# More portions of an edge-count matrix begun in the look-up turns of a graph-network kernel

## The chip, the cores and the metric

The kernel runs on one core of a Trainium2 chip. The metric is device time in microseconds (us) of one execution; the number given for a kernel is the median of several runs. The engines are named as in the profile: PE (TensorE, matrix multiplications; PEld is its weight load), DVE (VectorE), ACT (ScalarE), POOL (GpSimd) and SP (SyncE, which here only issues transfers). Each engine works through its own list of instructions in order and waits at an instruction until what it needs is there.

## What is computed

Four graph layers in a row over 6250 nodes with 64 features and 206,250 edges, each layer fed by a layer norm and a ReLU and added to its input. The edges come sorted by their destination.

```python
h = jnp.maximum(_layernorm(x, axis=-1), 0.0)
x = x + _L0_gnn_ref(h, edge_index, W3, b3, W4, b4)   # two normalized sums over neighbours, 64 -> 128 -> 64
h = jnp.maximum(_layernorm(x, axis=-1), 0.0)
x = x + _L1_gnn_ref(h, edge_index)                   # a normalized sum over neighbours
h = jnp.maximum(_layernorm(x, axis=-1), 0.0)
x = x + _L2_gnn_ref(h, edge_attr_64, src, dst, ...)  # messages per edge, gated by edge features
h = jnp.maximum(_layernorm(x, axis=-1), 0.0)
x = x + _L3_gnn_ref(edge_index, h)                   # three more normalized sums
```

The sum over neighbours, which most layers share, is

```python
deg = jax.ops.segment_sum(w, d, num_segments=n)
dinv = jnp.where(deg > 0, jax.lax.rsqrt(deg), 0.0)
msgs = (dinv[s] * dinv[d])[:, None] * x[s]
agg = jax.ops.segment_sum(msgs, d, num_segments=n)
```

## The kernel before

Nodes are padded to 6272, 49 blocks of 128. The kernel does not gather edge by edge: it builds once the dense matrix of edge counts, source by destination, in 8 bits, and every sum over neighbours is then a matrix product with it. The matrix is built in strips of destinations: 14 strips, alternately 512 and 384 destinations wide (`OF_CHUNK`). A strip stays in on-chip memory (pool `spool`, three buffers) until the first convolution has used it, and is written to main memory (`A`) for the later layers.

A strip is made of **portions** of 32 destinations: 16 portions in a wide strip, 12 in a narrow one, 196 in all. A portion takes two steps:

- `one_hots(s, q, n)` (L882, DVE): two comparisons (both L889), `hd` for the high part of the source and `lo` for its low part, against the keys of the edges that end in these destinations. `n` is 1 for a single portion or 2 for a pair made by one pair of instructions. The results lie in pool `opool`, two buffers.
- `placed(...)` (L896): for each portion sixteen matmuls on PE (L904) count the edges into `p_a` (two buffers of PSUM), and two copies on ACT (L908) put the counts into the strip. After a strip's last portion SP issues the write to `A` (L915).

`whole(s, q)` makes the one-hots of a single portion and puts it on the list `waiting`; `place()` takes all that wait through `placed`.

Everything happens in `first_stage`, where the order of the instructions on PE, DVE, ACT and POOL is the order of the code. It has these parts:

1. **Set-up.** Edge ends are read, packed into pairs (key, low part of the source) and written to main memory.
2. **The prelude**, a loop of 32 turns (L945), `GC` = 25 groups of 128 pairs of destinations running through it as in a pipeline. In turn i POOL issues the look-up `near` of group i (L948); DVE reads the look-up of group i-2 (L954) and finds the exact begin of its runs (L957); POOL issues the look-up `run` of group i-3 (L961); ACT copies the keys of group i-6 (L966) and turns group i-5 into digits (L973, L975), which PE transposes (L978); `place()` (L979) places what was made a turn earlier; after every ninth group and the last, DVE compares the keys (`less`, L987), PE counts them (L991) and DVE copies the counts (`below`, L994). At the end of a turn DVE fills in other work by a **credit** (L997 to L1002): so much credit is added per turn, and items are taken from the list `fill` and charged their cost until it is used up. The list holds the scans that find where each group begins (`scanned`, L866, with `begun_at`, L871) and the parts of the first layer norm (`centred`, `deviation`, `scaled`, L848 to L862). When it is empty, an item is one single portion of the first strip, at a cost of 2.0.
3. **The degrees.** After the loop DVE takes differences of `below` (L1007), PE spreads them (L1010), and from them comes the norm (L1018, L684 to L686). The portions not yet made become the list `jobs`; if their number is odd, one more single portion is made there.
4. **The scaled features**, in three 16-bit parts (`U3`, L1117 to L1124), while PE runs the first unit of the first convolution (L1129).
5. **The main loop** (L1150) over the pairs of portions in `jobs`: DVE makes the one-hots of the next pair while PE and ACT place the present one. After each portion `sums` hands out steps of the convolution (L1044) to PE. A step is one matmul of a block of a strip; there are 2401 steps in units of 98 or 49, and a unit may begin only when its destinations are built. How many steps follow a portion is what is left of them, divided by the portions left plus five. DVE reduces each finished unit (`added`, L1057), and the small operations of the hidden layer (`hidden`, L1078 to L1110) are spread between.

After the first stage come the gathers of the later layers (first matmuls at L1194), which read `A` back piece by piece, the edge stage, and the last layers.

The prelude's credit at L997 and its fallback at L999 read:

```python
credit += 1.4
while credit > 0:
    cost, f, *args = fill.pop(0) if fill else (2.0, whole, 0, singles)
    singles += f is whole
```

Of the kernel before, what the change touches and what calls it, by code (L numbers as in the profile page):

```python
# [593 lines left out]
CS = NP // CW  # L594
# [23 lines left out]
def fast(ctx, tc, bad, x, src, dst, edge_attr, W3, b3, W4, b4, w1, b1, w2, b2, Bw, Bb, Cw, Cb,  # L618
# [140 lines left out]
    def first_stage(ph):  # L759
# [115 lines left out]
        def portions(s):  # L875

            lo, hi = OF_CHUNK[s % 2]
            return (hi - lo) * P // 2 // (2 * SG)
# [43 lines left out]
        def place():  # L922
            while waiting:
                for _ in placed(*waiting.pop(0)):
                    pass
# [4 lines left out]
        fill = [(0.4, scanned, c) for c in range(3, 10)] + [(0.3, begun_at, 3, 10)]  # L930
# [11 lines left out]
        begun_at(0, 3)  # L942

        near_of, run_of, digits_of, credit, singles = {}, {}, {}, 0.0, 0
        for i in range(GC + 7):  # L945
            if i < GC:
                near_of[i] = rpool.tile([P, LOOK, 2], F32, name="near2")
                nc.gpsimd.indirect_dma_start(  # L948
                    out=near_of[i].rearrange("p e t -> p (e t)"), out_offset=None, in_=pairs[:, :],
                    in_offset=bass.IndirectOffsetOnAxis(ap=begin_i[:, i:i + 1], axis=0))  # L950
            if 0 <= i - 2 < GC:
                c = i - 2
                n = rpool.tile([P, 1], F32, name="n")
                nc.vector.tensor_scalar(junk[:, :LOOK], near_of.pop(c)[:, :, 0],  # L954
                                        start_of[:, c:c + 1], 0.0,
                                        op0=OP.is_lt, op1=OP.add, accum_out=n)
                nc.vector.tensor_add(exact_i[:, c:c + 1], begin[:, c:c + 1], n)  # L957
            if 0 <= i - 3 < GC:
                c = i - 3
                run_of[c] = rpool.tile([P, P, 2], F32, name="run")  # L960
                nc.gpsimd.indirect_dma_start(  # L961
                    out=run_of[c].rearrange("p e t -> p (e t)"), out_offset=None, in_=pairs[:, :],
                    in_offset=bass.IndirectOffsetOnAxis(ap=exact_i[:, c:c + 1], axis=0))
            if 0 <= i - 6 < GC:
                c = i - 6
                nc.scalar.activation(key[:, :, c * P:(c + 1) * P],  # L966
                                     digits_of.pop(c)[:, :2 * P].rearrange("p (k s) -> p k s", k=2),
                                     AF.Copy)
            if 0 <= i - 5 < GC:
                c = i - 5  # L970
                run = run_of.pop(c)
                digits = rpool.tile([P, 2, P], BF16, name="digits")
                nc.scalar.activation(digits[:, 0, :], run[:, :, 0], AF.Identity,  # L973
                                     bias=minus[:, c:c + 1])
                nc.scalar.activation(digits[:, 1, :], run[:, :, 1], AF.Copy)  # L975
                p = digits_of[c] = psum.tile([P, 1024], BF16, name="p_dig")
                for k in range(2):
                    nc.tensor.transpose(p[:, k * P:(k + 1) * P], digits[:, k, :], ident_b)  # L978
            place()  # L979
            if 0 <= i - 6 < GC:  # L980
                c = i - 6
                if c % 9 == 8 or c == GC - 1:
                    c0 = c // 9 * 9
                    p = psum.tile([P, 512], F32, name="p_node")
                    for k in range(3):
                        less = rpool.tile([P, 9 * P], BF16, name="less", bufs=2)
                        nc.vector.tensor_scalar(  # L987
                            less[:, :(c + 1 - c0) * P], key[:, 0, c0 * P:(c + 1) * P],
                            float(k * NB), None, op0=OP.is_lt)
                        for i_ in range(c0, c + 1):  # L990
                            nc.tensor.matmul(p[:, k * 9 + i_ - c0:k * 9 + i_ - c0 + 1],  # L991
                                             less[:, (i_ - c0) * P:(i_ - c0 + 1) * P],
                                             count[:, 1, 0:1], start=True, stop=True)
                    nc.vector.tensor_copy(  # L994
                        below[:, :, c0:c + 1],
                        p[:, :27].rearrange("p (k i) -> p k i", k=3)[:, :, :c + 1 - c0])
            credit += 1.4  # L997
            while credit > 0:
                cost, f, *args = fill.pop(0) if fill else (2.0, whole, 0, singles)  # L999
                singles += f is whole  # L1000
                f(*args)
                credit -= cost  # L1002
        assert singles <= portions(0) and not fill

        for h in range(2):
            at = slice(h * D, (h + 1) * D)
# [2 lines left out]
        for k in range(2):  # L1009
            nc.tensor.matmul(p[:, :2 * GC], spread_2[:, k, :],  # L1010
                             deg[:, k].rearrange("p h c -> p (h c)"), start=(k == 0), stop=(k == 1))
        jobs = [(s, q) for s in range(CS) for q in range(portions(s))][singles:]
        place()
        if len(jobs) % 2:
            whole(*jobs.pop(0))
# [156 lines left out]
    with ExitStack() as ph, tc.manual_schedule(  # L1172
            engines={ET.PE, ET.DVE, ET.Activation, ET.Pool}):
        norm0, norm3, V3, b4_r, hidden = first_stage(ph)
# [613 lines left out]
```

## Time and profile before

| | us |
|---|---|
| median of 3 runs | 3474.78 (3472.68 to 3476.98) |
| the profiled execution | 3475.05 |
| its span, first to last instruction | 3473.3 |
| DVE busy in the span | 2451.6 (71%) |
| PE busy in the span | 2702.6 (78%) |
| ACT / POOL busy in the span | 1228.0 / 1602.0 |

| place in the profiled execution | us from the span's start |
|---|---|
| first turn of the prelude on DVE | 23.98 |
| first single portion (L889) | 66.1 |
| degrees (L1007) | 104.93 |
| first pair's one-hots | 121.41 |
| DVE's last pair ends | 516.8 |
| first matmul of the gathers (L1194) | 527.46 |

The first stage takes some 527 of the 3473 us; what follows does not depend on the change but starts when the first stage lets it. Times on the timeline are microseconds from the start of the span; a bracket at the end of a line gives the idle time of that engine before the instruction and what ended it. An instruction's start may lie before the end of its forerunner on the same engine, as they are pipelined: the distance from start to start is what one costs.

### The profile page before, as it was taken

What the parts mean: (1) busy time and instruction counts of PE and PEld (TensorE: products, weight loads), DVE (VectorE), ACT (ScalarE), POOL (GpSimd) and SP (SyncE); (2) the same over time, 40 slices, a digit from 0 to 9 for tenths busy, and PEclk for the clock granted to TensorE, in tenths of its full rate; (3) what the DMA queues carried; (4) which work ended last, traced back from release to release, by engine and by line L of the source; (5) the groups of instructions that cost most, each with busy time, mean ns of one, the idle gap of its engine ahead of it and who ended that gap; (6) DMA issues with size and microseconds to landing.
All of it is one profiled execution on the core that took longest, in us unless ns stands there. A gap on an engine that the chain in (4) does not pass through costs nothing. (4 is left out here: it accounts for less than half of the span.)

```text
span 3473.3 us, 58582 instructions
## 1 busy us (share of the span) xinstructions
PE 2702.6 (78%) x23087; PEld 2113.6 (61%) x23087; DVE 2451.6 (71%) x4776; ACT 1228.0 (35%) x2071; POOL 1602.0 (46%) x1885
## 2 busy tenths in 40 slices
PE   1799999999966666776776777677677677699999
PEld 1688888999944444443443444444344344399999
DVE  6899993532268868978986997997898697641111
ACT  3677770000024433443444344444434344210000
POOL 6000001000047777777777777777777777500000
PEclk9999999999988888898888898899889989899999
DMA  4234347565443322332332333233233322346664
GB/s 134 64 80 109 83 105 254 188 212 178 147 130 91 87 55 69 91 82 70 97 86 79 88 94 82 76 94 82 67 96 90 79 70 79 85 161 200 204 207 146
DMA packets 255434, 389.54 MB, mean 112 GB/s; under 512 B 96409, under 2 KB 169289, under 8 KB 254894
## 3 DMA queue, kind: packets, MB, share of 16 engines
q1 hardware_dynamic: 190542, 320.69, 30.3%
q0 software_dynamic: 54816, 60.71, 8.4%
q10 hardware_dynamic: 9792, 4.31, 0.6%
q8 instruction: 184, 3.01, 0.3%
q14 instruction: 100, 0.82, 0.1%
HBM read 341.34 MB, written 44.21 MB: 111 GB/s over the span
## 5 line engine op out<-in xcount | busy, mean ns | idle before, releaser
L1527 POOL DMA_INDIRECT v<-Vp_dram,src_g x1616 | 1534.6, 950 | 885.0 <-issue 393.8
L1554 PE MATMUL p_bc<-BC,h 128*128 128x256 f32 x1616 | 512.5, 473 | 399.7 <-DVE m L1572 399.6
L1194 PE MATMUL p_acc<-U,piece 128*128 128x192 bf16 x9604 | 802.2, 247 | 2.5 <-DVE zg L1205 2.5
L1194 PEld LDWEIGHTS <-piece 128*128 128x128 fp8e4 x9604 | 796.3, 98 | 8.3 <-issue 7.7
L1554 PEld LDWEIGHTS p_bc<-BC,h 128*128 128x128 f32 x1616 | 363.8, 235 | 612.4 <-issue 511.6
L1205 DVE TENSOR_REDUCE zg<-p_acc 128x128 f32<-128x384 f32 x112 | 56.3, 507 | 494.8 <-PE p_acc L1194 494.3
L1438 DVE SCALAR_TENSOR_TENSOR junk<-p_sum,there 128x2048 bf16<-128x2048 fp8e4 (+1 forms) x112 | 361.9, 3232 | 8.8 <-PE p_sum L1433 8.6
L1580 ACT ACTIVATE m<-m 128x512 bf16<-128x512 f32 x202 | 127.2, 630 | 649.4 <-DVE m L1573 637.5
L908 ACT ACTIVATE strip<-p_a 128x784 fp8e4<-128x784 f32 x392 | 301.0, 821 | 95.5 <-PE p_a L904 87.6
L1571 DVE TENSOR_TENSOR m<-p_bc,v 128x512 f32<-128x512 f32 x202 | 139.4, 690 | 254.1 <-issue 103.2
L1586 DVE TENSOR_SCALAR to<-count,lane 128x128 bf16<-128x128 bf16 x1616 | 290.7, 276 | 0.0
L1594 PE MATMUL p_s<-m,to 128*128 128x192 bf16 x1616 | 195.0, 272 | 95.9 <-DVE H L1608 71.5
L1544 PE MATMUL p<-h,w_d 128*128 128x512 f32 x404 | 221.6, 631 | 60.5 <-ACT h L1548 60.5
L1548 ACT ACTIVATE h<-p,b_c 128x512 f32<-128x512 f32 x404 | 257.3, 695 | 3.8 <-PE p L1544 3.6
L1594 PEld LDWEIGHTS <-to 128*128 128x128 bf16 x1616 | 150.5, 109 | 168.8 <-DVE H L1608 106.5
L751 PE MATMUL p_sum<-piece,U 128*64 128x448 fp8e4 x2016 | 227.5, 366 | 31.6 <-DVE m L1656 25.7
L1561 DVE TENSOR_TENSOR p_bc<-p_bc,bias 128x1024 f32<-128x1024 f32 x202 | 247.5, 1225 | 2.3 <-PE p_bc L1554 1.8
L1566 ACT ACTIVATE p_bc<-p_bc 128x512 f32<-128x512 f32 x202 | 117.6, 582 | 342.6 <-DVE p_bc L1561 336.6
L1044 PE MATMUL p_sum<-U,strip 128*128 128x192 bf16 x2401 | 229.7, 247 | 0.0
L889 DVE TENSOR_TENSOR lo<-count,key 128x4096 bf16<-128x4096 bf16 (+1 forms) x103 | 224.4, 2179 | 0.0
L751 PEld LDWEIGHTS <-U 128*64 128x64 bf16 x2016 | 116.2, 113 | 167.2 <-issue 72.2
L1544 PE MATMUL p<-eT,w_d 128*128 128x512 f32 x404 | 214.7, 614 | 0.0
(206 smaller groups left out, 3081.0 us busy)
## 6 DMA issues: line engine op xcount, KB each, us to landing
piece<-A SPq DMA_DIRECT2D x243, 784.0 KB
e<-in_edge_attr SPq DMA_DIRECT2D x202, 256.0 KB
v<-Vp_dram,src_g POOLq DMA_INDIRECT x1616
A<-strip SPq DMA_DIRECT2D x7, 3136.0 KB
there<-A SPq DMA_DIRECT2D x196, 112.0 KB
A<-strip SPq DMA_DIRECT2D x6, 2352.0 KB
piece<-A SPq DMA_DIRECT2D x7, 448.0 KB
A<-strip ACTq DMA_DIRECT2D x1, 2352.0 KB
```

Of the source, the lines that this page charges most:

```text
L751: nc.tensor.matmul(p[half * D:(half + 1) * D, :w], U3[:, b, k, :], at_block, start=(i < 2), stop=(i >= 3 * n - 2))
L908: nc.scalar.activation(strips[s][:, :, col:col + 2 * SG].rearrange("p b (j l) -> p b j l", l=2), p[:, :, :2 * NB].rearrange("p j (b l) -> ...
L1044: nc.tensor.matmul(p[:, d * 3 * D:(d + 1) * 3 * D], strips[s][:, b, (d0 - lo + d) * P:(d0 - lo + d + 1) * P], U3[:, b, :, :].rearrange("p ...
L1194: nc.tensor.matmul(p[d // 2][:, d % 2 * 3 * D:(d % 2 + 1) * 3 * D], t[:, b, d * P:(d + 1) * P], U3[:, k * CB + b, :, :].rearrange("p t f - ...
L1438: nc.vector.scalar_tensor_tensor(junk[:m, :a1 - a0], p[:m, :a1 - a0, :].bitcast(COUNT).rearrange("p a (r j) -> p a r j", j=4), 15.5, of_th ...
L1527: ask = nc.gpsimd.indirect_dma_start(out=v[:, j, :], out_offset=None, in_=Vp_dram[:, :], in_offset=bass.IndirectOffsetOnAxis(ap=src_g[:, g ...
L1544: nc.tensor.matmul(of[g][p], w, of[g].pop(x), start=True, stop=True)
L1548: nc.scalar.activation(of[g][t], of[g].pop(p), **how)
L1554: last_of = nc.tensor.matmul(p_bc[:, 2 * q:2 * q + 2].rearrange("p j o f -> p (j o f)"), h2[:, q * P:(q + 1) * P], BC, start=True, stop=True)
L1561: nc.vector.tensor_tensor(p_bc, p_bc, bias.unsqueeze(1).to_broadcast([P, J, 2, D]), op=OP.add)
L1586: nc.vector.tensor_scalar(to[:, j, :], count, lane[:, g, j:j + 1], None, op0=OP.is_equal)
L1594: nc.tensor.matmul(p, to[:, j, :], m3[:, j].rearrange("p t f -> p (t f)"), start=(j == 0), stop=(j == J - 1))
```

## The change

The credit of a prelude turn goes from 1.4 to 2.0. The list of all portions, `jobs`, is made before the loop instead of after it, and the fallback item takes the next portion of this list, whichever strip it belongs to, where before it was always one of strip 0. After the loop the portions made are cut off the list as before. The bound in the assertion is widened to the first two strips.

```diff
         near_of, run_of, digits_of, credit, singles = {}, {}, {}, 0.0, 0
+        jobs = [(s, q) for s in range(CS) for q in range(portions(s))]
         for i in range(GC + 7):
...
-            credit += 1.4
+            credit += 2.0
             while credit > 0:
-                cost, f, *args = fill.pop(0) if fill else (2.0, whole, 0, singles)
+                cost, f, *args = fill.pop(0) if fill else (2.0, whole, *jobs[singles])
                 singles += f is whole
                 f(*args)
                 credit -= cost
-        assert singles <= portions(0) and not fill
+        assert singles <= portions(0) + portions(1) and not fill
...
-        jobs = [(s, q) for s in range(CS) for q in range(portions(s))][singles:]
+        jobs = jobs[singles:]
         place()
         if len(jobs) % 2:
             whole(*jobs.pop(0))
```

## The prediction

> **What bounds the kernel now.** I began with the busy table of the whole span, but its shares average stages with different limits, so the next view was the busy time by stretch, cut at the borders of the first stage. (Columns: the stretch, its length, then busy us and instruction counts of PE, PEld, DVE, ACT and POOL, the granted clock, the DMA share and GB/s.)
>
> ```profile
> core 0: us, PE busy (x) PEld busy (x) DVE busy (x) ACT busy (x) POOL busy (x), PEclk, DMA share, GB/s
> 24.00:66.00 42.00, 7.25 (x53) 3.58 (x53) 32.60 (x138) 15.97 (x51) 31.83 (x32) 1.00 0.30 87
> 66.00:105.00 39.00, 19.81 (x216) 15.76 (x216) 26.85 (x54) 23.69 (x54) 18.03 (x18) 1.00 0.20 59
> 105.00:121.40 16.40, 10.64 (x99) 9.97 (x100) 13.42 (x30) 9.49 (x17) 0.00 (x0) 1.00 0.00 1
> 121.40:516.90 395.50, 367.22 (x5322) 340.84 (x5320) 390.11 (x245) 298.01 (x399) 1.14 (x2) 0.98 0.38 95
> ```
>
> The main loop over pairs of portions (121.4 to 516.9) is DVE's: 390.1 of 395.5 us busy. In the prelude's turns with one-hots (66 to 105) no engine is full; DVE idles 12.2 of 39 us. So the change moves work from a place where DVE is the limit to one where something else is. What that is, the timeline of one turn shows (start, length, engine, line).
>
> ```profile
> 72.76 0.39 ACT L966 ACTIVATE key<-p_dig 128x256 bf16<-128x256 bf16 x1
> 73.02 0.42 ACT L973 ACTIVATE digits<-run,minus 128x128 bf16<-128x128 f32 x1
> ...
> 73.32 0.32 ACT L975 ACTIVATE digits<-run 128x128 bf16<-128x128 f32 x1
> ...
> 73.50 0.49 PE L978 MATMUL p_dig<-ident_b,digits 128*128 128x128 bf16 x2 [1.54 <-ACT digits L973]
> ...
> 73.78 1.51 PE L904 MATMUL p_a<-hd,lo 128*128 128x98 bf16 x16
> ...
> 74.67 1.54 ACT L908 ACTIVATE strip<-p_a 128x784 fp8e4<-128x784 f32 x2 [1.03 <-PE p_a L904]
> ...
> 76.10 0.39 ACT L966 ACTIVATE key<-p_dig 128x256 bf16<-128x256 bf16 x1
> ```
>
> The reader is to see a ring between ACT and PE: key and digits on ACT, the transposes and then the portion's sixteen matmuls on PE behind them, and ACT waiting 1.03 us for those before it evicts. From key to key it is 76.10 - 72.76 = **3.34 us a turn** wherever a portion is placed; a turn without a portion costs ACT only 1.28 (L973 at 76.36, then 77.64). DVE needs 2.45 for such a turn (its look-up reads start at 87.01 and 89.46, one single portion between), POOL 2 x 1.25 = 2.50 for its two look-ups (starts 73.19, 74.44). The ring ends the prelude:
>
> ```profile
> 100.72 0.39 ACT L966 ACTIVATE key<-p_dig 128x256 bf16<-128x256 bf16 x1
> ...
> 101.15 1.23 DVE L987 TENSOR_SCALAR less<-key 128x896 bf16<-128x896 bf16 x3 [3.69 <-ACT key L966]
> ...
> 102.92 0.97 DVE L889 TENSOR_TENSOR hd<-turns,key 128x1568 bf16<-128x1568 bf16 x1
> ```
>
> DVE sat 3.69 us for the last key; the degrees (L1007) follow at 104.93. In the main loop a pair's two comparisons stand back to back:
>
> ```profile
> 135.24 1.78 DVE L889 TENSOR_TENSOR hd<-turns,key 128x3136 bf16<-128x3136 bf16 x1
> 136.94 2.28 DVE L889 TENSOR_TENSOR lo<-count,key 128x4096 bf16<-128x4096 bf16 x1
> 139.15 1.78 DVE L889 TENSOR_TENSOR hd<-turns,key 128x3136 bf16<-128x3136 bf16 x1
> ```
>
> so a pair is 139.15 - 135.24 = **3.91 us** of DVE.
>
> **What changes, counted.** Walking the list of fills by its own costs: at 1.4 a turn the fills last through turn 17 and ten portions follow in turns 18 to 31, with four turns empty; at 2.0 they last through turn 12 and one portion follows in each of turns 12 to 31, twenty in all (16 of strip 0, 4 of strip 1). The main loop keeps 176 portions, 88 pairs instead of 93; an even number, so the extra single after the prelude stays out.
>
> *Main loop.* Five pairs go: 5 x 3.91 = -19.5 us. That all of it counts rests on DVE setting the pace. Test: the same reduction (L1057, the 64-wide one) starts at 243.48 and 302.82, 59.34 us apart for 14 pairs; 14 x 3.91 = 54.7, and the rest, 4.6, is what DVE's small operations in between take by their rows. Nothing is left over for waits, so PE and ACT are covered. The convolution's steps are handed out by the count of portions left; followed through, the last 40 portions receive the same numbers in both versions and 72 steps remain at the end in both, so the 10.5 us from DVE's last pair to the first gather (516.9 to 527.4) stay. At the loop's start the second unit needs 16 portions; today six portions pass without steps and DVE later waits 1.10 us at 144.23 behind PE. With 20 built the steps begin at once. That wait may go or merely move: bounds -1.1 and +1.1, taken 0.
>
> *Prelude, fills (turns 0 to 11).* Today POOL's 2.5 us a turn sets the pace; with more fills DVE does. DVE from 23.98, by steps from start to start: 22 scans x 0.39 = 8.6, two conversions 0.7, five centrings x 1.5 = 7.5 (45.07 to 46.55), six deviations x 0.55 = 3.3, seven scalings x 0.77 = 5.4, eleven look-up reads x 0.43 = 4.7, one single portion 2.02 (66.11 to 68.17 less waits: 0.89 + 1.13): turn 12 ends at 56.2, turn 13 at 58.7. Turn 14 compares keys (L987 to L994); the like of it took from 79.50 to 84.56, 5.1 us, at turn 23: DVE ends it near 63.7, its portion at 65.7, and ACT evicts that by 68.0.
>
> *Prelude, portions.* From turn 16 the ring sets the pace: 14 turns x 3.34 = 46.8 to turn 29. At turn 23 the comparisons hold DVE again: it is free 3.9 us after that turn's key (80.70 to 84.56 today), its portion 2.0 later, and the eviction 0.9 after that, at 6.8, where the ring wants it at 3.34 + 1.91 = 5.25: +1.5. So 68.0 + 46.8 + 1.5 = 116.3 for the last key. From it to DVE's next portion 2.20 (100.72 to 102.92), two portions now (turns 30 and 31, today only one) 4.04: the degrees at 122.5, against 104.93: **+17.6**. DVE's own waits for look-ups in the fills are not in it; today they are 1.5 us in every other turn (1.54 at 49.13, 1.55 at 54.40). None to three of them: 0 to 4.5, taken +0.4. So +18.0.
>
> *Moved with it.* ACT's evictions (2 x 0.72) and PE's sixteen matmuls of ten more portions are inside the 3.34. POOL's instructions are as many as before; the look-ups now have two ring turns, 6.7 us, from issue to use, against 2.8 from issue to first read (run at 29.73, digits at 32.53). SP's write of strip 0 (3136 KB) comes near 113 us instead of 139.54, behind the last look-up, with SP otherwise free until 520: nothing. Strip 1 starts in a third buffer that nobody holds: nothing. From the degrees to the first pair (16.5 us) the order is the same.
>
> **Sum:** +18.0 - 19.5 = -1.5 us. The profiled execution took 3475.05 us (span 3473.3), 0.3 above the median of 3474.78; on the median's scale **3473.3**. In words: DVE's idle time in the prelude is not filled, the turns stretch by about as much as is put into them.
>
> **Rivals.**
> 1. *PE gets quicker in the prelude* (faster). Sixteen matmuls take 1.51 us there, 0.91 at 145.10. With 0.91 the wait of 1.03 shrinks by about 0.45, on 14 turns 6.3, with turns 13 to 15 and the end 7: 3473.3 - 7 = 3466. For it: PE would have work in every turn for 60 us. Against: at the same density (turns 25 to 27, and 1.51 then 1.53 back to back at 98.40 and 100.18) they stayed at 1.5, as they were at 128 to 140 where the granted clock reads 0.50. The 1.00 in the prelude's clock column is therefore no evidence. [...] Chance 0.14.
> 2. *The ring is not what paces* (faster): turns at POOL's 2.50 from turn 16 on, 14 x 0.84 = -11.8: 3461.5. Against it stand six intervals of 3.33 to 3.35. Chance 0.08.
> 3. *Look-ups starve behind DVE's one-hots* (slower). POOL's look-up at 67.36, right after the first single portion, took 1.71 instead of 0.95, and ACT then waited 2.19 for digits. The lead of 6.7 us swallows this in the ring; before turn 12, where DVE and POOL are level, it would not: 12 turns x 0.76 = 9.1, giving 3482. [...] Chance 0.13.
> 4. *PE takes over the main loop* (slower). PE is busy 367 of 395.5 us there, and only 10 x 0.92 = 9.2 us of its work leaves, as the convolution's steps stay. If PE sets the pace once DVE has less, the gain is 9.2 instead of 19.5: 3473.3 + 10.3 = 3483.6. It decides when DVE's pair waits for a buffer that PE holds in most pairs; today that is 4.7 us over 93. For it: in the last ten pairs, with 16 to 19 steps a portion, DVE does wait (0.32, 0.57, 0.23). Against: the 59.34 above. Chance 0.15.
>
> The forecast has 0.50. Its own range, with the bounds named (-1.1 to +4.1, and 3 us for the two comparison turns), is 3468 to 3480. The range reaches to rivals 1 and 4: **3463 to 3485**, which leaves out rival 2 and the tails. A difference of 0.2%, 7 us, is about what a measurement tells from none: below 3467.8 lie most of rival 1, all of 2 and a trace of the forecast, 0.20; above 3481.7 most of 4, over half of 3, 0.20; between, 0.60.
>
> **What would show it.** Right: turns of 3.34 us between L966 starts from about 68 to 116; L1007 near 122.5; 88 pairs at 3.91; the distance from L1007 to the first gather matmul 19.5 shorter (now 527.46 - 104.93 = 422.5, then 403). Wrong: sixteen L904 matmuls below 1.2 us before 115 (rival 1); turns near 2.5 (rival 2); waits of ACT L973 on the run look-up in most turns (rival 3); L889's idle behind PE p_a above 10 us, or 14 pairs longer than 60 (rival 4).

## The result and the profile after

| | before | after |
|---|---|---|
| median | 3474.60 (8 runs, 3471.94 to 3476.98) | 3464.28 (8 runs, 3461.22 to 3467.38) |
| ratio | | 0.9972, 95% interval 0.9963 to 0.9981 |
| profiled execution (span) | 3475.05 (3473.3) | 3467.02 (3465.3) |

The changed kernel is 10.3 us faster, outside of the 0.2% and above the 1.5 us foreseen; 3464.28 lies inside the range, near its lower end. Lines of the changed kernel stand one higher than before from L946 on, as the diff adds a line. Followed along the timeline, the difference comes in two parts:

| place | before | after | difference |
|---|---|---|---|
| degrees (L1007, after L1008) | 104.93 | 121.05 | +16.1 |
| first pair's one-hots | 121.41 | 137.55 | +16.1 |
| DVE's last pair ends | 516.83 | 513.10 | -3.7 |
| first gather matmul (L1194, after L1195) | 527.46 | 523.75 | -3.7 |
| first reduction of the gathers (zg, L1205, after L1206) | 566.26 | 556.05 | -10.2 |
| last such reduction | 3465.1 | 3457.1 | -8.0 |

Up to the first gather matmul 3.7 us are won, which is what the portions themselves bring. Another 6.5 us appear within 40 us of the gathers, in code that the change does not touch; the rest of the kernel keeps them but for some 2 us in this pair of executions. The two parts are read one after the other.

**The first stage.** The busy time by stretch of the changed kernel, cut at the same borders as before (columns as there):

```profile
24.00:66.00 42.00, 10.56 (x97) 7.02 (x97) 37.09 (x131) 16.95 (x49) 30.81 (x30) 1.00 0.27 81
66.00:105.00 39.00, 20.83 (x225) 17.22 (x225) 30.10 (x62) 26.02 (x57) 20.21 (x21) 1.00 0.23 64
105.00:137.50 32.50, 19.77 (x205) 17.76 (x205) 24.05 (x43) 19.63 (x37) 0.00 (x0) 0.79 0.36 101
137.50:513.10 375.60, 354.94 (x5162) 330.20 (x5160) 370.44 (x235) 283.16 (x379) 1.15 (x2) 1.00 0.37 92
```

DVE still idles 8.9 of 39 us between 66 and 105, where it now makes a portion in every turn. The main loop shrank from 395.5 to 375.6 us and DVE fills it as before. The timeline of one prelude turn shows what holds DVE:

```profile
76.41 0.39 ACT L967 ACTIVATE key<-p_dig 128x256 bf16<-128x256 bf16 x1
...
77.15 0.50 PE L979 MATMUL p_dig<-ident_b,digits 128*128 128x128 bf16 x2 [1.55 <-ACT digits L974]
77.44 1.51 PE L904 MATMUL p_a<-hd,lo 128*128 128x98 bf16 x16
...
78.34 1.54 ACT L908 ACTIVATE strip<-p_a 128x784 fp8e4<-128x784 f32 x2 [1.03 <-PE p_a L904]
78.99 0.98 DVE L889 TENSOR_TENSOR hd<-turns,key 128x1568 bf16<-128x1568 bf16 x1 [0.76 <-PE p_a L904]
79.76 0.39 ACT L967 ACTIVATE key<-p_dig 128x256 bf16<-128x256 bf16 x1
```

From key to key it is 3.35 us, with the same wait of 1.03 on ACT, and DVE now waits for a buffer that PE still reads. The keys follow at 66.38, 69.72, 73.07 and so on to 93.15, then at 98.11 (a turn of 4.96 with the comparisons) and from there to the last at 114.84.

**Behind the first stage.** The timeline around the last portions and the first gathers, before (SPq and ACTq are the issues of transfers; their first number behind the start is how long the queue was at it):

```profile
519.22 0.90 PE L904 MATMUL p_a<-hd,lo 128*128 128x98 bf16 x16
520.15 4.87 SPq L1190 DMA_DIRECT2D piece<-A  x4
521.35 0.61 ACTq L915 DMA_DIRECT2D A<-strip  x1
522.00 15.79 ACTq L665 DMA_DIRECT2D pAw_d<-in_L_gnn_pAw  x1
531.94 4.21 PE L1194 MATMUL p_acc<-U,piece 128*128 128x192 bf16 x49
539.18 0.60 ACT L1086 ACTIVATE feat<-p_node 128x512 f32<-128x512 f32 x1 [17.86 <-issue]
539.83 2.07 PE L1091 MATMUL p_node<-feat,W3T 64*128 64x512 f32 x2 [3.69 <-ACT feat L1086]
542.68 2.07 PE L1091 MATMUL p_node<-feat,W3T 64*128 64x512 f32 x2 [0.78 <-ACT h L1093]
544.68 6.72 PE L1194 MATMUL p_acc<-U,piece 128*128 128x192 bf16 x49
```

and after:

```profile
510.75 0.91 PE L904 MATMUL p_a<-hd,lo 128*128 128x98 bf16 x16
511.68 10.01 SPq L1191 DMA_DIRECT2D piece<-A  x4
515.48 0.92 PE L904 MATMUL p_a<-hd,lo 128*128 128x98 bf16 x16
517.63 0.61 ACTq L915 DMA_DIRECT2D A<-strip  x1
518.27 11.96 ACTq L665 DMA_DIRECT2D pAw_d<-in_L_gnn_pAw  x1
531.65 0.60 ACT L1087 ACTIVATE feat<-p_node 128x512 f32<-128x512 f32 x1 [14.04 <-issue]
532.37 1.12 PE L1092 MATMUL p_node<-feat,W3T 64*128 64x512 f32 x2
534.27 1.12 PE L1092 MATMUL p_node<-feat,W3T 64*128 64x512 f32 x2 [0.78 <-ACT h L1094]
535.32 5.87 PE L1195 MATMUL p_acc<-U,piece 128*128 128x192 bf16 x49
```

Before, SP's first load of a piece goes out as the sixteen matmuls of the very last portion end (519.22 + 0.90 = 520.12, issue at 520.15). After, it goes out as those of the last but two end (510.75 + 0.91 = 511.66, issue at 511.68), with a whole pair still to come: 12.07 us ahead of the first gather matmul instead of 7.31. The last strip's write to `A` is issued by ACT, not by SP as the other strips' are (L915). Right behind it ACT is held, for 15.79 us before and 11.96 after, at the issue of a small load of a later stage, the second of the two of pAw_d (16 KB); `feat`, which ACT can compute only behind it, makes PE stand for 3.69 us before and not at all after. After the stop PE is slow, 6.72 us for 49 matmuls that took 4.21 ahead of it, and the granted clock reads 0.50 there (busy time by stretch, before):

```profile
530.00:535.00 5.00, 5.00 (x63) 4.99 (x61) 0.00 (x0) 0.00 (x0) 0.00 (x0) 1.00 1.16 291
535.00:540.00 5.00, 1.31 (x15) 1.08 (x14) 0.00 (x0) 0.60 (x1) 0.00 (x0) 0.96 0.79 175
540.00:545.00 5.00, 4.22 (x7) 1.13 (x8) 0.00 (x0) 0.90 (x2) 4.49 (x103) 0.50 0.83 292
545.00:550.00 5.00, 5.00 (x35) 4.76 (x32) 0.00 (x0) 0.47 (x1) 3.35 (x97) 0.51 1.04 308
```

In the changed kernel the granted clock falls too, to 0.50 from 536 to 539 and so for a shorter time, and with no wait of PE above 0.78 us in the gathers ahead of it:

```profile
535.00:540.00 5.00, 5.00 (x38) 4.52 (x38) 0.00 (x0) 0.69 (x1) 5.00 (x151) 0.66 1.02 377
```

The 6.5 us are accounted for on PE: the stop 3.69, the way from the first `feat` matmul to the next gather matmul 4.85 instead of 2.95 (1.90), and those 49 gather matmuls 6.72 instead of 5.87 (0.85; their forerunners took 4.21 in both), together 6.44.

Why the first piece may go earlier is to be seen in the addresses of the built kernels. The first piece takes bytes 114176 to 120448 of each partition. The two buffers for `lo` in `opool` begin at 113952 and 122144, 8192 bytes each, and are used in turn. With 10 singles and 93 pairs the last group's `lo` lies at 113952, on top of the first piece: that is 103 groups, an odd number. With 20 singles and 88 pairs, 108 groups, it lies at 122144, and the first piece waits only for the group before. This **theory A** (the turn of the buffers) had a rival, **B**: the 6.5 us come from the portions made early or from the first stage's new course. For the prelude the question was whether the ring of ACT and PE (**theory C**) is really what costs 16 us there, or whether its waits only stand where DVE or POOL would hold the turn anyway (**D**).

### The profile page after: what moved, and what is told of

It reads as the page before. It is cut to its first block, busy times and chain, and to the rows that moved or that the text cites. A ratio compares the mean times of both kernels' runs of the same rounds, so it can differ in the third digit from the quotient of the medians.

```text
span 3465.3 us, 58590 instructions
## 1 busy us (share of the span) xinstructions
PE 2698.9 (78%) x23087; PEld 2112.6 (61%) x23087; DVE 2450.9 (71%) x4786; ACT 1228.2 (35%) x2071; POOL 1606.7 (46%) x1885
## 5 line engine op out<-in xcount | busy, mean ns | idle before, releaser
L1195 PE MATMUL p_acc<-U,piece 128*128 128x192 bf16 x9604 | 802.1, 247 | 2.5 <-DVE zg L1206 2.5
L1195 PEld LDWEIGHTS <-piece 128*128 128x128 fp8e4 x9604 | 796.2, 98 | 7.5 <-issue 7.0
L1206 DVE TENSOR_REDUCE zg<-p_acc 128x128 f32<-128x384 f32 x112 | 56.3, 507 | 494.7 <-PE p_acc L1195 494.2
L904 PE MATMUL p_a<-hd,lo 128*128 128x98 bf16 x3136 | 193.4, 216 | 26.6 <-DVE lo L889 20.8
```

The source lines that it names most:

```text
L1195: nc.tensor.matmul(p[d // 2][:, d % 2 * 3 * D:(d % 2 + 1) * 3 * D], t[:, b, d * P:(d + 1) * P], U3[:, k * CB + b, :, :].rearrange("p t f - ...
```

## The experiments

The runs fell on other chips, on which the kernel before itself takes 3985 to 4010 us at a mean granted clock near 0.86 (0.925 in the profile shown), and its times spread over 40 us. So ratios are taken against runs of the kernel before on the same chip, and theories are judged by distances within a trace, which are steadier. The prelude of the kernel before is longer there (kernels with that prelude unchanged reach the degrees at 114.2 to 117.9, not 104.93), and in it DVE has waits of 1.6 to 5.3 us that end by something the trace does not name ("remote"): 7.2 to 14.4 us in all, where the first two profiles have none (e2, the changed kernel, has 4.9). What the change saves up to the first gather matmul is larger there: 6.2 us between e1 and e2.

**A first try at turning the buffers.** Two tiles of `opool` with a tiny write are taken after the prelude loop, to move the pairs on by one buffer; in the kernel before (e1) and in the changed one (e2).

```diff
+        for name, k in (("lo", 128), ("hd", 2 * NB)):
+            skipped = opool.tile([P, GB // GQ, k, GQ], BF16, name=name)
+            nc.vector.memset(skipped[:, 0, 0, :], 0.0)
```

> The kernel before with one more turn of the two-buffer pool of one-hots after the prelude (two tiles taken, one column of each cleared, nothing computed with them); the number of portions made early stays at ten. Theory A, the buffers: the last pair then lies in the other buffer, the buffer whose place the first pieces of the gathers take over is free one pair earlier, the first piece load is issued about 8 us earlier against the first gather matmul, PE's stop behind ACT's first copy of the last hidden layer (539.83) goes, and the time falls by 6.5 us, to about 3468; the first gather matmul itself stays at 527.5. Theory B, the earlier strips: what came after 523 us hangs on more portions having been made and written early; the time stays at 3474.6 within 2 us and the first piece load near 520.

> The changed kernel with the same additional turn of the pool of one-hots; twenty portions are still made early. Theory A: only the portions' own gain is left, first gather matmul at about 523.8 as in the changed kernel, but the first piece load moves from 511.7 to about 516.5 and the 6.5 us are lost again: about 3470.5, that is 3.7 to 4 below the kernel before. Theory B: stays at 3464.3 within 2 us.

The edit did not do what it was meant to: the addresses show the last `lo` where it had been (113952 in e1, 122144 in e2), as the spare tiles were free again before the next pair. So neither says anything on A against B. They serve as the two kernels on this chip: ratio 0.9987 [0.9963, 1.0011] and 0.9966 [0.9944, 0.9987]; from the first gather matmul to the first zg 38.60 and 30.64 us, 8.0 apart, where the first two profiles have 6.5.

**Two portions more, and an odd number of pairs.** The changed kernel with a credit of 2.1: 22 portions early, 87 pairs, last `lo` at 113952.

```diff
-            credit += 2.0
+            credit += 2.1
```

> The changed kernel with a credit of 2.1: 21 portions in the prelude's turns and one more after it, 22 early, 87 pairs; the pool of one-hots has turned 109 times, an odd number as in the kernel before (103), where the changed kernel has 108. Theory A: the portions give about 1 us, the odd number takes back 6.5: about 3470. Theory B: a little below the changed kernel, 3463 within 2 us.

Ratio 0.9976 [0.9950, 1.0002]. Against e2 on the same chip the first gather matmul comes 2.0 us earlier, the first zg 4.8 us later: the distance is 37.43 us again, the piece load 7.31 us ahead. More portions early, and the 6.5 us are lost. B does not allow that.

**The buffers turned for good.** The first pair of the main loop is made as two singles, so the groups are one more and everything else stays: in the kernel before (e5), in the changed one (e6), and with two pairs split as a control (e7).

```diff
-        ready = one_hots(*jobs[0], 2)
+        groups = [(j, 1) for j in jobs[:2]] + [(j, 2) for j in jobs[2::2]]
+        ready = one_hots(*groups[0][0], groups[0][1])
...
-        for k in range(0, len(jobs), 2):
-            coming = one_hots(*jobs[k + 2], 2) if k + 2 < len(jobs) else None
+        for k in range(1, len(groups) + 1):
+            coming = one_hots(*groups[k][0], groups[k][1]) if k < len(groups) else None
```

> The kernel before, with the first pair of the main loop made as two single portions: 94 comparisons' groups instead of 93 there, so the last pair's `lo` lies in the other buffer (at byte 122144 instead of 113952), out of the way of the first piece at 114176. The number of portions in the prelude stays at ten. Cost: two singles at 2.02 for a pair at 3.91, +0.15 us. Theory A (the turn of the two buffers decides when the first piece may be loaded): piece load about 12 us ahead of the first gather matmul instead of 7.3; from the first gather matmul to the first zg reduction about 31 us instead of 38.5; the time 6 to 8 us below the kernel before. Rival B (the 6.5 us come from the portions made early, or from anything else of the change): 7.3 and 38.5 unchanged, the time within 1 us of the kernel before.

> The changed kernel with the same split of the main loop's first pair: 89 groups instead of 88, so the last `lo` lies at 113952 as in the kernel before; twenty portions in the prelude as in the change. Theory A: piece load about 7.3 us ahead of the first gather matmul instead of 12.1, from there to the first zg 37 to 38.5 us instead of 30.6; the time 6 to 8 us above the changed kernel, that is 2 to 4 us below the kernel before. Rival B: 12.1 and 30.6, the time 10 us below the kernel before.

> The changed kernel with its first two pairs split: 90 groups, so the buffers stand as in the changed kernel, at twice the price of the split (+0.3 us). Theory A: 12.1 us and 30.6 us as in the changed kernel, about 10 us below the kernel before and 6 to 8 below the kernel with one split. If the split itself cost the time (rival B's way out): slower than with one split.

The timeline of the kernel before with one split (e5):

```profile
525.28 33.80 SPq L1191 DMA_DIRECT2D piece<-A  x11
531.89 11.96 ACTq L665 DMA_DIRECT2D pAw_d<-in_L_gnn_pAw  x1
537.37 4.21 PE L1195 MATMUL p_acc<-U,piece 128*128 128x192 bf16 x49
545.25 0.60 ACT L1086 ACTIVATE feat<-p_node 128x512 f32<-128x512 f32 x1 [14.03 <-issue]
545.98 1.12 PE L1091 MATMUL p_node<-feat,W3T 64*128 64x512 f32 x2
```

and of the changed kernel with one split (e6):

```profile
524.93 31.52 SPq L1192 DMA_DIRECT2D piece<-A  x10
526.78 15.96 ACTq L665 DMA_DIRECT2D pAw_d<-in_L_gnn_pAw  x1
532.24 4.21 PE L1196 MATMUL p_acc<-U,piece 128*128 128x192 bf16 x49
544.14 0.60 ACT L1087 ACTIVATE feat<-p_node 128x512 f32<-128x512 f32 x1 [18.04 <-issue]
544.79 2.07 PE L1092 MATMUL p_node<-feat,W3T 64*128 64x512 f32 x2 [3.87 <-ACT feat L1087]
```

The two have changed places. The kernel before has got the early load, the hold of 11.96 us and no stop of PE, without one portion more in its prelude; the changed one has got the late load, the hold of 15.96, the stop and the slow matmuls. To the first zg it is 30.64 us in e5, 38.72 in e6, and 32.30 in e7, where the buffers stand well again at twice the price of the split. Theory A holds. The times go the same way but with wide intervals, that of e5 reaching past 1: e5 0.9982 [0.9959, 1.0004], e6 0.9961 [0.9942, 0.9980], e7 0.9949 [0.9926, 0.9972]; the medians of e6 and e7 are 9.6 us apart, where 6 to 8 were expected. That e6 would be only 2 to 4 us below the kernel before was missed, its median is 13.4 below; 5 to 7 us of that show in the trace, where its first gather matmul at 532.2 stands against 537.4 in e5 and 539.5 in the next kernel, both with the old prelude. e7's median is 23.0 below the kernel before, where about 10 was expected. The rest of both lies inside the spread of the times, so it is the distances that bear theory A out.

**Where the late load is paid.** The kernel before, buffers left in the bad order, but with the small loads of the second stage (pAw_d and pBw_d) issued by POOL instead of ACT.

```diff
-    def diagonal(m, name, pool=const):
+    def diagonal(m, name, pool=const, by=nc.scalar):
...
-            nc.scalar.dma_start(t[k * D:(k + 1) * D, k * D:(k + 1) * D], m)
+            by.dma_start(t[k * D:(k + 1) * D, k * D:(k + 1) * D], m)
...
-        pAw_d = diagonal(pAw, "pAw_d", wpool)
-        pBw_d = diagonal(pBw, "pBw_d", wpool)
+        pAw_d = diagonal(pAw, "pAw_d", wpool, nc.gpsimd)
+        pBw_d = diagonal(pBw, "pBw_d", wpool, nc.gpsimd)
```

> The kernel before, with four small loads of the second stage (pAw_d and pBw_d, 16 KB each) issued from POOL's queue instead of ACT's. The buffers stay in the bad order, the piece load stays 7.3 us ahead. Theory A1 (the late release is paid through ACT: its issue of a small load is held for 15.8 us behind the transfers, feat is late, PE stops 3.7 us and its clock falls to half): ACT is free, feat follows the last portion within 2 us, PE's stop is gone, from the first gather matmul to the first zg 31 to 34 us instead of 38.5, the time 4 to 7 us below the kernel before. Theory A2 (it is paid at the pieces themselves, which come late for PE): PE's stop moves to the pieces, 37 to 38.5 us, the time within 1.5 us of the kernel before.

```profile
531.98 28.12 SPq L1190 DMA_DIRECT2D piece<-A  x8
539.50 4.22 PE L1194 MATMUL p_acc<-U,piece 128*128 128x192 bf16 x49
...
544.25 0.60 ACT L1086 ACTIVATE feat<-p_node 128x512 f32<-128x512 f32 x1 [11.09 <-PE p_node L1083]
548.12 1.12 PE L1091 MATMUL p_node<-feat,W3T 64*128 64x512 f32 x2
551.08 4.22 PE L1194 MATMUL p_acc<-U,piece 128*128 128x192 bf16 x49
```

The piece load is as late as before (7.52 us ahead), yet PE runs through: `feat` now waits for PE's transposes (L1083) and not for the queue, and the 49 matmuls behind it take 4.22. 30.65 us to the first zg, 7 to 8 less than in the kernels with the late load and ACT held; ratio 0.9961 [0.9940, 0.9982]. (The medians are 16.6 us apart, more than the 4 to 7 expected and more than the trace shows.) So PE does not lack the pieces; the late load is paid through ACT, which stands at the issue of a 16 KB load that nothing needs soon (A1, not A2). Why that issue is held 4 us longer when the pieces are loaded later was not separated.

**The ring of the prelude.** In the changed kernel PE does the sixteen matmuls of a waiting portion before the turn's two transposes instead of after them. ACT's order stays. (`counted_early` and `evicted_early` are `placed` cut in two, its matmuls and its copies.)

```diff
+            early = [counted_early(*waiting.pop(0)) for _ in range(len(waiting))]
             if 0 <= i - 5 < GC:
...
                 for k in range(2):
                     nc.tensor.transpose(p[:, k * P:(k + 1) * P], digits[:, k, :], ident_b)
-            place()
+            for at_ in early:
+                evicted_early(*at_)
```

> The changed kernel with PE's sixteen matmuls of a waiting portion put ahead of the turn's two transposes in PE's order, ACT's order unchanged (keys, digits, then the two evictions). Theory C, the ring of ACT and PE sets the turn: ACT no longer waits 1.03 us for the portion's matmuls, the turns from 16 to 29 fall from 3.34 to the 2.5 us of POOL's two look-ups, the prelude ends 11 us earlier (degrees near 110) and the time is about 3453. Rival D, DVE with its 2.45 us and its waits for look-ups sets the turn, the ring only follows: the turns stay above 3.1 and the time is at 3462 or above.

The last keys on ACT's timeline:

```profile
105.00 0.39 ACT L992 ACTIVATE key<-p_dig 128x256 bf16<-128x256 bf16 x1
107.45 0.39 ACT L992 ACTIVATE key<-p_dig 128x256 bf16<-128x256 bf16 x1
109.90 0.39 ACT L992 ACTIVATE key<-p_dig 128x256 bf16<-128x256 bf16 x1
112.08 0.42 ACT L992 ACTIVATE key<-p_dig 128x256 bf16<-128x256 bf16 x1
114.26 0.44 ACT L992 ACTIVATE key<-p_dig 128x256 bf16<-128x256 bf16 x1
```

These are turns of 2.18 to 2.45 us with a portion in each, where the change had 3.35: C holds, D does not. Ten of the fourteen turns from turn 16 to the last key are between 2.1 and 2.8 us; the other four, two of them at the second comparison of the keys, take 3.2 to 6.3 us, so the mean is 3.03, against 3.64 in e2. The degrees come at 120.50 against 129.57 in e2 on the same chip, 9.1 us earlier where 11 were expected, and the whole 9.1 us arrive at the first gather matmul (523.17 against 532.27) and the first zg (553.82 against 562.91). Ratio 0.9922 [0.9893, 0.9952]: faster than the kernel before, and its median of 3952.49 is 21 us below that of e2, of which the trace shows the 9.1.

**How much of it is left.** The same order with 28 portions (credit 2.5, 84 pairs, good buffers), with the ten of the kernel before (credit 1.4), and the changed kernel as it is beside them.

> PE's sixteen matmuls ahead of the transposes as in e3_matmuls_ahead, and 28 portions made in the prelude instead of 20 (2.5 a turn); 84 pairs follow, an even number, so the buffers stand in the good order. Theory P (with the ring broken, DVE is what a turn with a portion waits for, so eight more portions cost it there what four pairs save): the prelude 12 to 16 us longer, four pairs or 15.6 us less behind it, the first gather matmul within 3 us of that kernel's (523.2), the time within 5 us of it. Rival Q (DVE still has idle time in the prelude to give): the prelude only 6 to 10 us longer, the first gather matmul 6 to 9 us earlier, the time as much lower.

> PE's sixteen matmuls ahead of the transposes, but with the ten early portions of the kernel before (1.4 a turn) and its 93 pairs, so the last `lo` lies in the bad place. Theory P (the ring of ACT and PE is what a portion costs in the prelude; six turns of 3.34 go to about 2.5): the degrees 4 to 6 us earlier than in the kernel before, the first gather matmul as much; the first zg still 37 to 39 us behind it; the time 4 to 6 us below the kernel before. Rival Q (the ring cost nothing while only ten portions were there): the time within 1 us of the kernel before.

> The changed kernel as it is, for a time and a trace beside the other two. Both theories: the degrees near 129, the first gather matmul near 532, the first zg 31 to 32 us behind it, the time 10 to 15 us below the kernel before.

28 portions: ratio 0.9929 [0.9904, 0.9954]; degrees at 132.41, 11.9 us later than with 20, and the first gather matmul at 523.31, as with 20 (523.17 on another chip; the changed kernel gives 532.27 and 532.32 on these two). What the prelude takes, the main loop gives back: with the ring gone, more portions early are worth nothing. The changed kernel: 0.9973 [0.9952, 0.9994], degrees at 129.65, first zg 30.64 us behind the first gather matmul. Ten portions: 0.9996 [0.9970, 1.0023], and the 4 to 6 us expected are missed. Its turns are 2.45 us near the end (102.07, 104.52, 106.97), but the degrees at 114.62 are only level with the best of the kernels with the old prelude, and the time is near what rival Q said. Most of DVE's waits for key comparisons there are of the kind named above, ended by "remote":

```profile
96.13 0.46 DVE L1015 TENSOR_SCALAR less<-key 128x1152 bf16<-128x1152 bf16 x1 [4.55 <-remote]
```

They come to 16.3 us on DVE in this profile, against 7.2 in e5, 10.2 in e1 and 14.4 in e8, which have the old prelude. What they are stays open, and as they vary by more than the 4 to 6 us looked for, this one profile settles nothing. So the ring is shown to set the turns, and to cost where every turn has a portion; that it costs with ten portions is not shown.

All kernels by what decides behind the first stage (us; `lo` at byte; "ahead" is from the first piece load's issue to the first gather matmul):

| kernel | portions early | last `lo` at | ahead | ACT held | first gather matmul to first zg |
|---|---|---|---|---|---|
| before | 10 | 113952 | 7.31 | 15.79 | 38.80 |
| e1 | 10 | 113952 | 7.31 | 15.95 | 38.60 |
| e4 | 22 | 113952 | 7.31 | 15.91 | 37.43 |
| e6 | 20 | 113952 | 7.31 | 15.96 | 38.72 |
| e10 | 10 | 113952 | 7.31 | 15.90 | 38.67 |
| after | 20 | 122144 | 12.07 | 11.96 | 32.30 |
| e2, e3, e11 | 20 | 122144 | 12.08 | 11.91 to 11.96 | 30.64 to 30.65 |
| e5 | 10 | 122144 | 12.09 | 11.96 | 30.64 |
| e7 | 20 | 122144 | 12.09 | 11.99 | 32.30 |
| e9 | 28 | 122144 | 12.09 | 11.93 | 32.29 |
| e8, small loads on POOL | 10 | 113952 | 7.52 | none | 30.65 |

## Why the prediction was right, and where it was not

- **The ring, turns of 3.34 us.** Right: 3.35 from key to key, the wait of 1.03, turn 23 longer by 1.6 (foreseen 1.5); and e3 shows that it is the cause of the long turns.
- **Prelude +18.0.** Right in kind, 1.9 too large. From the last key to the degrees it is 6.21 us, as foreseen (122.5 - 116.3), but the last key came at 114.84 and not at 116.3. As the turns are as foreseen, this 1.5 lies in the estimate of the fills ahead of the ring: the key of turn 16, from which the ring was counted, was put at 68.0 and came at 66.38. The other 0.4 is what was added for DVE's waits for look-ups. Of these the prelude has one left, 1.1 us, where there were six with 8.4; so without waits the fills were put some 2.7 us too long.
- **Main loop -19.5.** Right: -19.9 from the first pair to the last, and 402.7 us from the degrees to the first gather matmul, foreseen 403. DVE's waits for PE there are as before, 4.6 us in ten places against 4.7 in nine (line below).
- **"The 10.5 us from DVE's last pair to the first gather ... stay."** Right as it stands: 523.75 - 513.10 = 10.65.
- **The step that failed** is the next one, which was not worked out: that all behind it only shifts. SP was said to be "otherwise free until 520", but what it waits for at 520 was not asked, and the buffers that the pieces are laid on were not looked at. An odd number of groups became an even one, and with it the wait of the first piece went one group back. This term, put at nothing by silence, is 6.5 us, more than the whole net effect of the portions, -3.7.
- **Rival 1, PE quicker in the prelude**: fell. The sixteen matmuls take 1.51 us at 77.44 and still at 105.83, though PE had a portion in every turn and was idle at most 1.55 us at a time in the ring; its stretches of work there are 1.8 us (77.15 to 78.95). What keeps them at 1.51 us there, while the granted clock's column reads 1.00, was not shown. Where 0.50 is read, the length of the gap alone does not decide: the stop of 3.69 us is followed by 0.50, but in the changed kernel 0.50 is read too, from 536 to 539, and no wait of PE in the gathers ahead of it is longer than 0.78 us.
- **Rival 2, the ring not the pacer**: fell by the turns. **Rival 3, look-ups starving**: fell, as the waits for look-ups became fewer (ACT's for the `run` look-ups went from 18.0 us to 0.8). **Rival 4, PE taking over the main loop**: fell; DVE's waits for PE there did not grow, and 370.4 of 375.6 us are DVE's.
- **The range.** The forecast had "no change" as likeliest. Its own range, 3468 to 3480 (the bounds that it names add up to 3469.2 to 3480.4), holds what the portions alone give, 3474.6 - 3.7 = 3470.9, but not the measured 3464.28. The wider range held it only because its lower end reached out to rival 1, which did not come true: that was luck.

The waits of DVE on PE in the main loop of the changed kernel (us in total, times, longest):

```profile
DVE hd L889 <- PE p_a L904: 4.6, 10, 0.6
```

## What to carry to other kernels

A change that alters how many times a rotating buffer is used alters which of its copies is used last, and what the next stage lays on that place then waits one round more or less (here the first piece load went out 7.31 or 12.07 us ahead of the first gather matmul): look at the addresses and at the first transfer of the next stage, not only at the work that is moved. Where an engine with work on the critical path also issues transfers, a small load that nobody needs soon can hold that engine for longer than the work takes, as it did ACT here, for 11.9 to 16.0 us ahead of a `feat` of 0.60; put it on a queue whose engine is idle (with the loads on POOL's queue, e8, it was 30.65 us from the first gather matmul to the first zg, against 38.80 in the kernel before). And before work is moved into idle time, ask what makes the idle time: here putting a portion's matmuls ahead of two transposes on PE (9.1 us) was worth more than ten portions made early behind them (3.7 us up to the first gather matmul, 6.2 us on the chip where the 9.1 were measured).

## What the runs showed of the hardware that was not expected

- ACT stood 11.9 to 16.0 us at the issue of a 16 KB load right behind the issue of a 2352 KB write on the same queue, in each kernel where that load was ACT's.
- PE at some 54% load (1.80 of 3.35 us a turn), with gaps of no more than 1.55 us, stayed at 1.49 to 1.53 us for sixteen matmuls (0.91 in the main loop) for the 50 us of the ring, while the granted clock's column reads 1.00 for these stretches. In the kernel before, a stop of 3.69 us in full work was followed by 0.50 for some 10 us (540 to 549).
- With the same good order and the same waits, the 49 matmuls behind `feat` took 4.22 us in e2, e3, e5 and e11 and 5.87 in the changed kernel, e7 and e9: these 1.65 us are the difference between the 30.64 and 32.30 in the table. In the changed kernel the granted clock reads 0.50 for some 3 us of these matmuls (536 to 539). Why they are slow in these three and not in the other four, behind the same wait of 0.78 us, was not found.
